# A graph layer and a mixture of experts on one core: the second expert's weights queued behind the fourth node tile's row instead of the first's

## Chip, cores, metric

One NeuronCore of a Trainium2 chip runs the whole program in one launch. The metric is the device time of that launch in microseconds; lower is better. The time before is the median of 3 runs.

## What is computed

625 nodes with 512 features pass a relational graph layer and then a mixture of 16 experts, each with a residual. Cut to what matters:

```python
def gnn(x, heads, tails, rel):               # x = layernorm(input), [625, 512]
    H = einsum('rod,nd->rno', W_rel, x) + b_rel     # 16 relations
    agg = segment_sum(H[rel, tails], heads) + segment_sum(H[rel + 8, heads], tails)
    return relu(x @ W_self.T + b_self + agg)

def moe(x):                                  # x = layernorm(input), [625, 512]
    logits = x @ router_w.T                  # 16 experts
    vals, idx = top_k(logits, 2)
    w = softmax(vals)
    return sum_e w[:, e] * ((silu(x @ gate_w[e]) * (x @ up_w[e])) @ down_w[e])

x = x + gnn(layernorm(x), src, dst, edge_type)
x = x + moe(layernorm(x))
```

There are 10625 edges. One expert has gate and up weights of 512 by 1024 and down weights of 1024 by 512, all float32: 2 MB each, 6 MB together.

## The kernel before

**Node tiles.** The nodes are cut into five tiles of 128 rows, numbered 0 to 4. The graph stage first makes two tables of messages, `h_tab`, with 80 products for each (`relation`, L256), and sorts the edges. Then 128 messages at a time, a chunk, are fetched by index: GpSimd (POOL) issues the indirect DMA at L547 or L553, and TensorE (PE) adds a chunk into its tile with a zero-and-one matrix `to`. Most chunks are split into two parts first (L591 to L595). The last 17 chunks, named `whole` in the code (L614), are multiplied unsplit at L587: three for each of tiles 0 to 3, and five for tile 4. These 17 are the last gathers of the graph stage.

**Finishing a tile.** `finish` (L607) adds the residual (L609, VectorE or DVE), normalizes the row (L148 to L165), stores the normalized tile to `hn_rows` on ScalarE's DMA queue (L611) and stores the tile of `out` on SyncE's (SP's) queue (L612). It keeps that last instruction in the list `stored`. Tiles finish in the order 0, 1, 2, 3, 4. The generator `rest(j)` then routes a tile: four transposes (`pT`, L691), a copy (`hT`, L693), the product with the router (`pl`, L700), the two best experts, and the places of the tile's pairs (L716 to L760). A list of steps written by hand interleaves `finish` and `rest` (L894).

**Experts.** Pairs of a token and an expert are packed into units of 32 tokens. A unit gets its rows by an indirect DMA from `hn_rows`, is transposed on DVE (L788), and runs through gate and up on PE (L800, 32 matmul records for each unit) to `sil` on ScalarE (L812) and `hid` on DVE. The down product is L837, and an indirect DMA adds the result into `out` (L862). Experts 0, 1 and 2 come first, with three units each, called o00, o01, o10, o11, o20, o21, o02, o12, o22 below: the first digit is the expert, the second the unit; PE takes them in this order. Their rows are fetched at L768 by `get_first`: the six of units 0 and 1 once tiles 0 to 3 are routed, the three of unit 2 once tile 4 is. Thirteen more experts follow, in an order found at run time.

**Weights.** Three sets of buffers (`wts0`, `wts1`, `wts2`) take turns, each of 6 MB. `load_hidden` (L173 to L199) and `load_expert` issue three DMAs from SP for an expert: gate, up, down. Expert 0 is loaded during the graph stage. Expert 1 goes to `wts1`, room that the sorting of the edges leaves. Expert 2 goes to `wts2`, room that the graph stage leaves: its load waits until the stage's readers are through, among them the stores of `out` (L612) and `hn_rows` (L611) and the router's last product. Each later expert waits for PE to be done with the set it replaces.

**What sets the place of a load in SP's queue.** `load` takes an instruction from the list `early`, if there is one, and is put behind it by `tc.issue_after`; a scheduler does the rest. Before, `early.extend(3 * stored)` stands ahead of the step list, when `stored` holds tile 0's store alone: expert 1's three loads come right behind it. SP's queue runs in order, and a DMA that SP is to issue can wait for the landing of an older one.

Of the kernel before, what the change touches and what calls it, by code (L numbers as in the profile page):

```python
# [22 lines left out]
NT = 5  # L23
# [51 lines left out]
def kernel(  # L75
# [96 lines left out]
    early = []  # L172

    def load_hidden(e):


        pool = wts[0]
        wts.append(wts.pop(0))

        def load(t, w):  # L180
            s = w[e] if isinstance(e, int) else w[ds(e, 1)].rearrange("o k f -> (o k) f")
            behind = tc.issue_after(early.pop(0)) if early else nullcontext()
            with behind:
                nc.sync.dma_start(t, s.rearrange("(k p) f -> p k f", p=P))

        wgu = pool.tile([P, KD, 2, F], F32, name="wgu")
        load(wgu[:, :, 0, :], gate_w)
        load(wgu[:, :, 1, :], up_w)

        def load_output():  # L190
            wd = pool.tile([P, KF, D], F32, name="wd")
            load(wd, down_w)
            return wd

        return wgu, load_output

    def load_expert(e):
        wgu, load_output = load_hidden(e)
        return wgu, load_output()  # L199
# [3 lines left out]
    with gnn:  # L203
# [401 lines left out]
        stored = []  # L605
# [11 lines left out]
        def add(j, n):  # L617
            for _ in islice(adding[j], n):
                pass
# [46 lines left out]
        weights0 = load_expert(0)  # L666
# [89 lines left out]
        def told_first(units, pairs, all):  # L756

            for c in range(*pairs):
                nc.tensor.matmul(
                    pw0[:, units, :], at[:, c, :], tok0[:, c, units, :], start=(c == 0), stop=(c == all - 1)  # L760
                )

        def get_first(units, tiles):

            nc.vector.tensor_scalar(get0[:, units], pw0[:, units], quarter, 0.0, op0=ALU.add, op1=ALU.max)
            for s in range(NS):
                for g in range(SU)[units]:
                    nc.gpsimd.indirect_dma_start(  # L768
                        out=xb0[:, g, s, :], out_offset=None, in_=hn_quarters[: tiles * P * NQ],
                        in_offset=bass.IndirectOffsetOnAxis(ap=get0[:, g, s : s + 1], axis=0),  # L770
                    )
# [116 lines left out]
        for j in (1, 2, 3):  # L888
            add(j, 3)
        add(0, 3)  # L890

        early.extend(3 * stored)
        weights = [weights0, load_expert(1)]
        for step in ((1, 3), 0, 0, (2, 3), 1, 0, 1, 0, (3, 3), 2, 1, 2, 1, (4, 3), 3, 2, 3, 2, (4, 1), 3, 3):  # L894
            if isinstance(step, int):
                next(tiles[step])
            else:
                add(*step)
        get_first(slice(0, SA), NT - 1)
        told_first(slice(SA, SU), (0, 2 * NT - 2), 2 * NT)  # L900

# [530 lines left out]
```

## Time and profile before

| | |
|---|---|
| median of 3 runs | 725.66 us (722.46 to 725.88) |
| profiled execution, its time | 728.91 us |
| profiled execution, its span | 726.9 us (2.0 us less than its time) |
| PE busy | 676.6 us (93%) |
| DVE busy | 409.0 us (56%) |
| POOL busy | 292.1 us (40%) |
| ScalarE busy | 112.8 us (16%) |
| DMA | 201.13 MB, mean 277 GB/s |
| chain that ended last | PE 74%, DMA 7%, POOL 7%, nothing visible 6% |
| load of gate weights, issue to landing | 19.6 us median |
| L553 gather, issue to landing | 5.3 us median |

The span reaches from the first to the last event of the profiled execution. Matmul ends are modelled and some records are missing, so a PE that is shown busy is not PE at its peak. "Granted clock" is the share of full speed that PE's throttle granted. A timeline row gives start, duration, engine, line, operation and tiles; behind `<-` stands what ended the idle time before it. "Issue to landing" of a DMA counts from the issuing instruction to the DMA's completion.

The stretch that the change touches runs from about 400 us to 480 us: the 17 gathers, the five tiles' finish and routing, and the nine units of experts 0 to 2.

### The profile page before, as it was taken

To read this page: it belongs to the slowest core of one execution; us is meant where nothing else is said; L and a number is where in the kernel's file an instruction comes from. 1 tells how busy PE (TensorE), PEld (TensorE's weight loads), DVE (VectorE), ACT (ScalarE), POOL (GpSimd) and SP (SyncE) were. 2 spreads that over 40 slices of the span, in tenths; PEclk is the share of its full clock that TensorE was granted. 3 is DMA by queue.
4 is the path that set the end of the run, shared out by engine and by line. 5 is a ranking of instruction groups with operands and counts; after the bars stand their busy time and mean duration, and the time that the engine had idled before them with its cause. 6 is when DMAs were issued, how large, how long until landed. Compare 5 with 4: busy or idle time off the path is not lost.

```text
span 726.9 us, 9984 instructions
## 1 busy us (share of the span) xinstructions
PE 676.6 (93%) x3509; PEld 301.4 (41%) x3509; DVE 409.0 (56%) x1106; ACT 112.8 (16%) x218; POOL 292.1 (40%) x263
## 2 busy tenths in 40 slices
PE   4999999999959999999999797999999999999991
PEld 2444444444425555455555253233333333333340
DVE  6569986899249987576887564862222222122210
ACT  2100000000014433233433112111100010001010
POOL 1000004777877770477774713134442222111021
PEclk9999999999979999999999886999999999999996
DMA  7075746999989983689976797579999999999971
GB/s 234 15 270 225 258 144 176 247 269 265 209 257 293 309 271 148 208 270 302 329 244 195 239 404 256 220 268 356 396 383 386 382 395 388 394 396 394 397 253 22
DMA packets 81384, 201.13 MB, mean 277 GB/s; under 512 B 9544, under 2 KB 10226, under 8 KB 81328
## 3 DMA queue, kind: packets, MB, share of 16 engines
q1 hardware_dynamic: 46400, 125.57, 46.4%
q0 software_dynamic: 21712, 52.27, 27.5%
q10 hardware_dynamic: 13216, 22.59, 8.3%
q8 instruction: 29, 0.48, 0.3%
q14 instruction: 27, 0.22, 0.1%
HBM read 175.58 MB, written 27.85 MB: 280 GB/s over the span
## 4 chain that ended last, share of the span: by engine, by line
PE 74%; DMA 7%; POOL 7%; issue 6%; DVE 3%; ACTq 1%; ACT 1%; POOLq 0%; DVEq 0%
PE o L256 25%; PE o L800 24%; PE y L837 12%; POOL agg L547 6%; DMA g<-h_tab,rows 4%; PE m L595 4%; PE m L594 3%; PE m L587 2%; PE ps L494 1%; DMA h_tab<-hs 1%; DMA agg<-h_tab,rows 1%; PE pl L700 1%; DMA wt<-in_w_rel 1%; PE m L564 1%; ACTq L234 1%
## 5 line engine op out<-in xcount | busy, mean ns | idle before, releaser
L256 PE MATMUL o<-wt,xT 128*128 128x512 f32 x680 | 308.4, 599 | 0.7 <-ACT xT L247 0.7
L256 PEld LDWEIGHTS o<-wt,xT 128*128 128x128 f32 x680 | 127.7, 192 | 137.1 <-issue 131.7
L800 PE MATMUL o<-wgu,xbT 128*32 128x512 f32 x1600 | 179.2, 600 | 0.0
L553 POOL DMA_INDIRECT g<-h_tab,rows x142 | 143.6, 1011 | 75.2 <-issue 28.4
L547 POOL DMA_INDIRECT agg<-h_tab,rows x40 | 64.6, 1614 | 133.0 <-DVE off L442 114.1
L591 ACT CAST hi<-g 128x512 fp32r<-128x512 f32 x125 | 71.8, 618 | 224.7 <-DMA g<-h_tab,rows 126.1
L593 DVE TENSOR_TENSOR lo<-g,hi 128x512 fp32r<-128x512 f32 x125 | 82.3, 692 | 35.7 <-ACT hi L591 34.0
L800 PEld LDWEIGHTS o<-wgu,xbT 128*32 128x32 f32 x1600 | 51.8, 111 | 120.8 <-issue 120.4
L788 DVE STREAM_TRANSPOSE xbT<-xb 128x128 f32<-128x128 f32 x50 | 15.1, 307 | 146.7 <-PE o L800 131.2
L837 PE MATMUL y<-wd,hidT 128*32 128x512 f32 (+2 forms) x608 | 92.7, 516 | 0.0
L325 DVE TENSOR_TENSOR hs<-o,bt 128x512 f32<-128x512 f32 x80 | 55.0, 689 | 43.3 <-PE o L256 34.5
L594 PE MATMUL m<-hi,to 128*128 128x512 f32 x125 | 63.5, 508 | 10.0 <-ACT hi L591 10.0
L950 POOL DMA_INDIRECT xb<-hn_rows,get x41 | 39.5, 963 | 57.2 <-DVE xbT L788 32.6
L837 PEld LDWEIGHTS y<-wd,hidT 128*32 128x32 f32 (+2 forms) x608 | 38.7, 128 | 52.1 <-issue 43.9
L595 PE MATMUL m<-lo,to 128*128 128x512 f32 x125 | 55.2, 441 | 1.7 <-DVE lo L593 1.7
L862 POOL DMA_INDIRECT out<-ys,adds x10 | 15.6, 1559 | 76.9 <-ACT ys L857 55.8
L812 ACT ACTIVATE sil<-o 128x256 f32<-128x256 f32 x50 | 19.2, 384 | 150.9 <-PE o L800 146.5
L490 DVE TENSOR_TENSOR val<-oc,vals 128x564 f16<-128x564 f16 (+1 forms) x56 | 38.7, 725 | 0.0
L594 PEld LDWEIGHTS m<-hi,to 128*128 128x128 f32 x125 | 23.9, 191 | 23.8 <-ACT hi L591 13.1
L817 DVE SCALAR_TENSOR_TENSOR hid<-sil,weight,o 128x256 f32<-128x256 f32 x41 | 19.7, 481 | 24.4 <-ACT sil L812 20.7
L595 PEld LDWEIGHTS m<-lo,to 128*128 128x128 f32 x125 | 23.9, 191 | 18.0 <-DVE lo L593 8.9
L474 DVE TENSOR_TENSOR at<-count_h,slot_p 128x768 f16<-128x768 f16 x28 | 26.8, 957 | 0.0
(251 smaller groups left out, 375.5 us busy)
## 6 DMA issues: line engine op xcount, KB each, us to landing
wgu<-in_gate_w SPq DMA_DIRECT2D x16, 2048.0 KB, 19.6
wgu<-in_up_w SPq DMA_DIRECT2D x16, 2048.0 KB, 21.1
wd<-in_down_w SPq DMA_DIRECT2D x16, 2048.0 KB, 23.4
h_tab<-hs ACTq DMA_DIRECT2D x80, 256.0 KB, 4.7
wt<-in_w_rel SPq DMA_DIRECT2D x16, 1024.0 KB, 12.1
bt<-in_b_rel SPq DMA_DIRECT2D x16, 256.0 KB, 12.4
g<-h_tab,rows POOLq DMA_INDIRECT x142, 5.3
xs<-in_x SPq DMA_DIRECT2D x5, 256.0 KB, 5.2
```

The costliest lines, as they stand in the source:

```text
L256: nc.tensor.matmul(o, xT[:, k, ts(j, P)], wt[:, k, :], start=(k == 0), stop=(k == KD - 1))
L325: nc.vector.tensor_tensor(hs, linear(wt, j), bt, ALU.add)
L490: nc.vector.tensor_tensor(val[:, :, i, :], oc, vals[:, cs, i : i + 1].to_broadcast([P, SG, n_ch]), ALU.mult)
L547: nc.gpsimd.indirect_dma_start(out=agg[:, ts(c % NT, D)], out_offset=None, in_=h_tab[d][: n * NP, :], in_offset=at, bounds_check=n * NP - ...
L553: nc.gpsimd.indirect_dma_start(out=g, out_offset=None, in_=h_tab[d][: n * NP, :], in_offset=at,)
L591: nc.scalar.copy(hi, g)
L593: nc.vector.tensor_tensor(lo, g, hi, ALU.subtract)
L594: nc.tensor.matmul(m, at, hi, start=first, stop=False)
L595: nc.tensor.matmul(m, at, lo, start=False, stop=last)
L800: last = nc.tensor.matmul(o[ts(c, Q), :].rearrange("p (s m i) -> p s m i", s=2, i=Q), xbT[:, k, :], wgu[:, k].rearrange("p s (m c i) -> p ...
L837: nc.tensor.matmul(y[at * Q : (at + m) * Q, : cols.stop - cols.start], hidT[:, k, u * Q : (u + m) * Q], wd[:, k, cols], start=(k == 0), st ...
L950: nc.gpsimd.indirect_dma_start(out=xb, out_offset=None, in_=hn_quarters, in_offset=bass.IndirectOffsetOnAxis(ap=get, axis=0),)
```

## The change

Expert 1's loads are no longer traced ahead of the step list. They are traced inside it, once `stored` holds four stores, and are put behind the last of these, tile 3's:

```diff
-
-        early.extend(3 * stored)
-        weights = [weights0, load_expert(1)]
+        weights = [weights0]
         for step in ((1, 3), 0, 0, (2, 3), 1, 0, 1, 0, (3, 3), 2, 1, 2, 1, (4, 3), 3, 2, 3, 2, (4, 1), 3, 3):
             if isinstance(step, int):
                 next(tiles[step])
             else:
                 add(*step)
+            if len(stored) == NT - 1 and len(weights) == 1:
+
+                early.extend(3 * stored[-1:])
+                weights.append(load_expert(1))
```

In the built programs the order of instructions on PE, DVE, ScalarE and POOL is the same. SP's queue alone differs. Before: store of tile 0, gate, up and down of expert 1, stores of tiles 1 to 4, gate, up and down of expert 2. After: stores of tiles 0 to 3, gate, up and down of expert 1, store of tile 4, gate, up and down of expert 2. Some DMAs share a completion semaphore with other ones than before: the stores of tiles 1 to 3 no longer wait for a load of expert 1.

## Prediction

> **What bounds the kernel now.** I read the page first (PE busy 93% of the span), then the chain of work that ended last. From 445 us the chain is PE almost without a break to the end, and the DMA queue's waits say that the later experts' loads wait for PE. So what moves is when PE can run its first nine units. The chain just ahead of them:
>
> ```profile
> 409.35 9.28 DMA g<-h_tab,rows
> 418.68 2.07 PE m L587 x2
> ...
> 445.44 11.27 PE o L800 x80
> 456.85 22.45 PE o L800 x208
> ```
>
> A gather of 256 KB holds PE for 9.28 us. The issue-to-landing times of the L553 gathers, first those issued at 404 to 406 us, then those at 414 to 420 us:
>
> ```profile
> L553 POOL DMA_INDIRECT g<-h_tab,rows x2: 946/1021/1096, 404.2 to 405.6; - x2
> ...
> DMA to landing us min/median/max: 4.8/4.8/4.8
> ...
> L553 POOL DMA_INDIRECT g<-h_tab,rows x5: 942/946/946, 414.4 to 419.4; - x5
> ...
> DMA to landing us min/median/max: 10.6/10.9/11.7
> ```
>
> What came between is in SP's timeline: expert 1's 6 MB.
>
> ```profile
> 407.19 0.36 SPq L612 DMA_DIRECT2D out<-xs  x1
> 408.20 0.38 SPq L184 DMA_DIRECT2D wgu<-in_gate_w  x1
> ...
> 444.01 0.39 SPq L184 DMA_DIRECT2D wgu<-in_gate_w  x1
> 444.45 0.50 SPq L184 DMA_DIRECT2D wgu<-in_up_w  x1
> ```
>
> The table by stretches (the last three columns are granted clock, DMA share, GB/s) shows the same from PE's side: starved, then throttled.
>
> ```profile
> 404.00:408.00 4.00, 3.70 (x9) 1.23 (x8) 2.00 (x5) 0.00 (x0) 2.99 (x3) 1.00 0.60 185
> 408.00:414.00 6.00, 2.08 (x4) 0.42 (x4) 3.23 (x11) 0.31 (x2) 4.68 (x5) 0.92 0.88 275
> 414.00:420.00 6.00, 5.07 (x6) 1.77 (x7) 0.00 (x0) 0.28 (x1) 4.46 (x6) 0.50 0.99 355
> ```
>
> The nine units end one by one at ScalarE's `sil`; the fifth, o20, is the first that needs expert 2:
>
> ```profile
> 462.20 0.38 ACT L812 ACTIVATE sil<-o 128x256 f32<-128x256 f32 x1 [3.05 <-PE o L800]
> 465.63 0.38 ACT L812 ACTIVATE sil<-o 128x256 f32<-128x256 f32 x1 [3.05 <-PE o L800]
> ```
>
> So o20 starts at 462.2. Expert 2's up weights, issued at 444.45, land 16.5 us later (issue-to-landing of that one DMA), at 460.95: only 1.25 us ahead of their use. That small slack decides this case.
>
> **What is removed: the load beside the gathers.** POOL issues the 17 gathers at most 1.25 us apart, whatever the load does. Tile 3's last is the twelfth, issued at 413.11. Uncontended it lands 4.8 us later, at 417.9; its two matmuls take about 1 us (1.13 in the row at 407.83), so tile 3's L609 starts at about 419.3, where it now starts at 425.99: 6.7 us earlier. The bound from below is 3.3 us of landing (the fastest of this stretch: 1.5 us more gain), from above the 9.9 us of the gathers issued near it now (no gain). The value is near the 4.8 of 404 to 406 us, where the DMA share is 0.60. The stores of tiles 1 to 3 move into this time: 0.8 MB. They now wait behind the load (13.6 us of SP's queue for the gate load's landing); afterwards they go as their tiles finish. In the 0.40 of DMA time left, 0.8 MB at 400 GB/s is 2 us of some 13: I cost it at nothing; if it isn't hidden, 1 us.
>
> From tile 3's L609 to tile 4's the trace has 9.85 us (425.99 to 435.84), from there to the first L800 9.5 us (to 445.4). Both are routing in an unchanged instruction order. So PE would be ready for o00 at 419.3 + 9.85 + 9.5 = 438.7.
>
> **What is added: the load beside tile 4 and the first units' rows.** Tile 3's store goes out at about 420.1; gate follows 1.0 us later, as at 407.19 and 408.20; bytes flow from about 422.
> - Tile 4's last gather, issued at 419.37, would land at 424.2 alone and at 431.1 with today's worst 11.7 us. PE reaches it at 434.5 - 6.7 = 427.8. Two or three gathers overlap the load, not ten, so I take 427: cost 0, upper end 3.3 us.
> - The six row gathers of L768, issued now from 440.19 when the queues are nearly empty, landed 2.6 us later (the first). They move to 433.5, into the load. In the stage with 388 GB/s the same kind of gather lands in 6.1 us (median, 520 to 640 us); those beside the start of expert 2's load took 7.9. I take 6.3: 439.8, and o00 at 440.3 instead of 445.4. Of 6.7 us 5.1 are left; by 7.9 us it would be 3.5.
> - Each unit still takes 3.43 us, and o00 its half-clock start. So PE would want o20 at 462.2 - 5.1 = 457.1. Expert 1 itself, wanted at about 450 by o10, is in by then.
>
> **Expert 2, moved by this without being touched.** Its gate load is issued at 444.01, released by the router's last product; SP waited 5.2 us for the store of `hn_rows` just before. It also needs tile 4's store of `out` landed. Now that one takes 5.1 us, issued at 436.6. Afterwards it stands behind expert 1's 6 MB in the same queue. [...] By the 5.1 us, expert 2 would be issued at pl's end, 444.0 - 6.7 = 437.3, and hold nothing: gain 5.1. [...] That end: at 422 there are 6.3 MB of load, 0.6 of gathers, 0.8 of `hn_rows` and 0.4 of rows to move, 8.1 MB; at 400 GB/s (the trace has 400 to 406 from 420 to 438 us) 20.3 us, with a slow start 1 us more: 443.3. The store's 0.26 MB and its completion make 1.5 us, so gate goes out at about 445.0, 1 us later than now. Bounds: 442, if tile 3 comes earlier, and 448.5, if the six small gathers cost the queues 0.8 us each, as they seem to near 450 us.
>
> Up follows 0.4 us later. Now it takes 16.5 us, with three row gathers beside it; two times 2.1 MB at 400 GB/s are 10.5 us, with start and completion 13. The gathers will be through, so I take 15, between them: it lands at 460.4. PE, ready at 457.1, waits 3.3 us, and o20 starts 1.8 us earlier than today.
>
> **After o20** nothing is late: the third rows hang on DVE work behind o10, the next expert's gate load waits 16.5 us for PE at 472.50, and DMA share is 0.03 from 466 to 472 us. Gain and loss at o20 reach the end one to one. On the profiled execution (span 726.9, time 728.91) the sum is 727.1; that one lies 3.25 us above the median, so on the median 725.66 - 1.8 = 723.9.
>
> **Rivals.**
> 1. *Expert 2 is no hindrance.* Its load, with no gathers beside it, lands by 457 (issue 443.5, 13 us). For it: 13 us is what the bytes ask. Against it: today's 16.5. The gain is 5.1 us: 720.6. Chance 0.22.
> 2. *The wait before o20 costs the clock (slower).* [...] A unit then takes 6.9 instead of 3.43 us; half clock over 5 to 10 us loses 2.5 to 5 us. It decides once up lands after about 461 (gate issued after 446). With o20 at 461.7 and 4.5 us lost, 4 us slower: 729.7. Chance 0.20.
> 3. *The gathers don't get faster*, because stores and half a clock hold the tiles, not the load. Then tile 3 stays near 426, the load ends at about 449, up lands near 466, o20 is 3.5 us late: 729.2. The jump from 4.8 to over 10 us right at the load speaks against it. Chance 0.08. That the loads don't move at all is excluded by SP's built order.
>
> **How the numbers follow.** The main case has 0.50. Its own range, from up landing at 458.6 to 463.2, is 722.1 to 726.7. Half a per cent, 3.6 us, is about what a measurement of this kernel can tell from no change. Faster by more than that: rival 1 and the main case's early edge, 0.26. Slower: the larger halves of rivals 2 and 3, 0.19. Within: 0.55. The range reaches from 719.8 (rival 1, tile 3 a little earlier) to 729.0 (the middle of rivals 2 and 3).
>
> **What would show it.** Right: L553 gathers at about 5 us up to 416 us; L609 of tile 3 at 419 to 420 and tile 4 at 429; granted clock full in 414 to 420; first L800 at 440 to 441; tile 4's store landing some 14 us after its issue; expert 2's gate issued at 444 to 446; a PE wait ahead of o20. Wrong: gathers still at 9 us; expert 2's gate at 438 (rival 1 or better); clock 0.50 after 457 (rival 2). A stall elsewhere, such as PE waiting for expert 1 at o10, would make the whole sum wrong.

## The result, and the profile after

The changed kernel takes 729.82 us (median of 15 runs, 726.73 to 731.81). The kernel before took 725.66 us beside it (15 runs, 722.46 to 729.3). The ratio is 1.0052, with an interval of [1.0035, 1.0069]: slower by about 3.8 us (the medians differ by 4.2). The prediction was 723.9 us.

The upper half of the change did what it was meant to do. The L553 gathers of the changed kernel, first those issued at 404 to 413 us, then those at 413 to 418:

```profile
L553 POOL DMA_INDIRECT g<-h_tab,rows x8: 942/946/947, 404.1 to 412.9; - x8
...
DMA to landing us min/median/max: 4.5/4.6/5.0
...
L553 POOL DMA_INDIRECT g<-h_tab,rows x5: 942/946/947, 412.9 to 417.9; - x5
...
DMA to landing us min/median/max: 5.2/5.5/5.8
```

They land in about half the time: the later ones in 5.5 us (median) instead of 10.9. In the table by stretches (columns as before: stretch, its length, busy times of PE, PEld, DVE, ACT and POOL, then granted clock, DMA share, GB/s) PE is busy 4.52 us of the six in which it had been starved, and keeps its full clock:

```profile
408.00:414.00 6.00, 4.52 (x13) 1.88 (x14) 2.61 (x7) 0.29 (x1) 4.59 (x5) 1.00 0.86 284
414.00:420.00 6.00, 5.19 (x23) 2.65 (x22) 4.38 (x22) 1.47 (x3) 3.78 (x4) 1.00 0.95 320
```

The gain is then lost at one place. ScalarE's `sil` marks the end of each unit; o11, the last that needs no weights of expert 2, and o20, the first that does:

```profile
455.47 0.38 ACT L812 ACTIVATE sil<-o 128x256 f32<-128x256 f32 x1 [3.05 <-PE o L800]
468.24 0.38 ACT L812 ACTIVATE sil<-o 128x256 f32<-128x256 f32 x1 [12.39 <-PE o L800]
```

o11 ends 6.7 us earlier than before, o20 2.6 us later (1.5 us of both is that this execution came to tile 0 sooner, see below). PE's timeline splits these 12.8 us into a wait of 6.5 and a unit that takes 6.3 in place of 3.4:

```profile
439.11 10.87 PE L800 MATMUL o<-wgu,xbT 128*32 128x512 f32 x80 [0.87 <-DVE xbT L788]
...
450.04 5.36 PE L800 MATMUL o<-wgu,xbT 128*32 128x512 f32 x48
461.92 18.27 PE L800 MATMUL o<-wgu,xbT 128*32 128x512 f32 x144 [6.52 <-DVE hid L815]
```

The releaser named in the last row is doubtful: `hid` of o11 ended at 461.80, but the up weights of expert 2 landed at 461.78 (the last of the trace's semaphore marks for that DMA), and in the profiles below the same row names `in_up_w`. In g2, below, o20 starts at 453.93, though `hid` of o11 ends only at 458.26: it does not wait for it. Short stretches around the wait show the clock:

```profile
453.40:457.00 3.60, 2.00 (x20) 0.39 (x12) 0.98 (x3) 0.38 (x1) 1.17 (x1) 1.00 1.06 394
457.00:460.40 3.40, 0.00 (x0) 0.00 (x0) 2.63 (x9) 0.00 (x0) 0.00 (x0) 1.00 1.04 267
460.40:463.80 3.40, 1.88 (x12) 0.65 (x16) 1.95 (x4) 0.00 (x0) 0.00 (x0) 0.50 0.93 349
463.80:467.20 3.40, 3.40 (x24) 0.88 (x19) 0.00 (x0) 0.00 (x0) 0.00 (x0) 0.50 0.38 146
```

And SP's timeline shows why expert 2 is late:

```profile
405.71 14.13 SPq L612 DMA_DIRECT2D out<-xs  x4
420.03 0.39 SPq L184 DMA_DIRECT2D wgu<-in_gate_w  x1
420.48 0.60 SPq L184 DMA_DIRECT2D wgu<-in_up_w  x1
...
429.35 4.78 SPq L612 DMA_DIRECT2D out<-xs  x1
445.20 0.37 SPq L184 DMA_DIRECT2D wgu<-in_gate_w  x1
445.62 0.50 SPq L184 DMA_DIRECT2D wgu<-in_up_w  x1
```

Four stores, then expert 1's load, then tile 4's store at 429.35, and expert 2's gate only at 445.20. What SP waited for just before it (us in total, times, longest), and that one store's issue-to-landing:

```profile
SPq L184 <- DMA out<-xs: 5.6, 1, 5.6
```

```profile
L612 SPq DMA_DIRECT2D out<-xs x1: 4776/4776/4776, 429.4 to 429.4; - x1
...
DMA to landing us min/median/max: 15.6/15.6/15.6
```

**How profiles are compared here.** One execution differs from the next by a few us. Two things make the traces comparable. From the ninth `sil` to the end of the span every profile below, those of a slower chip left out, has 247.3 to 247.9 us, so nothing differs there. And tile 0's L609, ahead of which nothing of the change lies, starts anywhere from 402.9 to 408.2 us. What matters is the stretch between these two points: 72.9 us before, 77.0 after, which is 4.1 us more; of these the span shows 2.5, because the profiled execution of after happened to reach tile 0 1.5 us sooner.

### The profile page after: what moved, and what is told of

Its sections match the earlier page's. It is cut to its first block, busy times and chain, and to the rows that moved or that the text cites. A ratio compares the mean times of both kernels' runs of the same rounds, so it can differ in the third digit from the quotient of the medians.

```text
span 729.4 us, 9981 instructions
## 1 busy us (share of the span) xinstructions
PE 678.3 (93%) x3509; PEld 301.3 (41%) x3509; DVE 409.0 (56%) x1106; ACT 111.9 (15%) x218; POOL 292.8 (40%) x263
## 5 line engine op out<-in xcount | busy, mean ns | idle before, releaser
L800 PE MATMUL o<-wgu,xbT 128*32 128x512 f32 x1600 | 181.6, 606 | 7.4 <-DVE hid L815 6.5
L553 POOL DMA_INDIRECT g<-h_tab,rows x142 | 143.6, 1011 | 76.2 <-issue 27.4
L800 PEld LDWEIGHTS o<-wgu,xbT 128*32 128x32 f32 x1600 | 52.4, 112 | 130.1 <-issue 121.4
L862 POOL DMA_INDIRECT out<-ys,adds x10 | 15.6, 1559 | 76.7 <-ACT ys L857 55.7
L490 DVE TENSOR_TENSOR val<-oc,vals 128x564 f16<-128x564 f16 (+1 forms) x56 | 38.5, 720 | 0.0
```

The costliest lines, as they stand in the source:

```text
L490: nc.vector.tensor_tensor(val[:, :, i, :], oc, vals[:, cs, i : i + 1].to_broadcast([P, SG, n_ch]), ALU.mult)
L553: nc.gpsimd.indirect_dma_start(out=g, out_offset=None, in_=h_tab[d][: n * NP, :], in_offset=at,)
L800: last = nc.tensor.matmul(o[ts(c, Q), :].rearrange("p (s m i) -> p s m i", s=2, i=Q), xbT[:, k, :], wgu[:, k].rearrange("p s (m c i) -> p ...
```

## The experiments

My theory after the result: expert 2's load waits for tile 4's store, which stands behind expert 1's 6 MB in SP's queue; the load lands late; PE's wait then halves the clock. The rivals: something else holds expert 2 (the row gathers of the third units, which now fall into its load, or the chip's limit), or the clock is innocent.

| run | edit to the changed kernel | median us (runs) | ratio to before | stretch us | PE's wait ahead of o20, us |
|---|---|---|---|---|---|
| after | none | 729.82 (15) | 1.0052 [1.0035, 1.0069] | 77.0 | 6.52 |
| g1 | none, again | 731.70 (7) | 1.0058 [1.0026, 1.0091] | 74.6 | 4.60 |
| e1 | tile 4's store on ScalarE's queue | 720.12 (11) | 0.9937 [0.9907, 0.9966] | not used | |
| g2 | the same, again | 722.99 (7) | 0.9941 [0.9914, 0.9968] | 68.5 | 0.76 |
| e3 | third units' rows later | 727.58 (22) | 1.0028 [1.0011, 1.0045] | 72.2 | 2.82 |
| g4 | store and rows | 720.55 (6) | 0.9908 [0.9886, 0.9930] | 67.6 | 0.38 |
| e2 | o20 filled twice | 730.14 (8) | 1.0055 [1.0029, 1.0081] | 77.1 | none |
| g3 | o20 filled once | 727.78 (12) | 1.0022 [0.9997, 1.0048] | 72.2 | 1.34 |
| e4 | the kernel before, store on ScalarE's queue | 726.31 (14) | 1.0010 [0.9984, 1.0036] | 71.6 | none |

The e runs shared one chip (before: 725.79 us, 42 runs), the g runs another (726.17 us, 19 runs). By their profiles the stretch of one kernel scatters by 2.4 us (77.0 and 74.6 for the changed kernel), so the ratios carry the verdicts and the traces the reasons.

**Take the store out of SP's queue (e1, g2).**

```
-            stored.append(nc.sync.dma_start(out[ts(j, P), :], xs[:, j, :]).ins)
+            queue = nc.scalar if j == NT - 1 else nc.sync
+            stored.append(queue.dma_start(out[ts(j, P), :], xs[:, j, :]).ins)
```

> The kernel after, with tile 4's store of out issued on ScalarE's DMA queue instead of SP's. Theory (expert 2's load waits for this store, which stands behind expert 1's 6 MB; PE then waits at o20 and its clock halves): the store lands by 440, expert 2's gate is issued at 438 to 440 instead of 445.2, its bytes follow expert 1's without the gap of 444 to 447, up lands at 456 to 458 instead of 461.8, o20 starts there at full clock; 719.5 to 721.5 us. Rival (the loss lies elsewhere, in the gathers or later among the thirteen experts): expert 2 comes earlier, but the time stays within 2 us of 729.8.

Measured 0.9937: faster than both kernels by this one line. The profiled execution of e1 took 730.1 us, ten over its median, so its trace is not read. The trace is that of g2, the same kernel again:

> The changed kernel with tile 4's store of out on ScalarE's queue, to have its trace in an ordinary run. My theory: expert 2's gate is issued at 440 to 442 (tile 4's hn_rows is then what SP waits for), in_up_w lands before 458, no idle time of TensorE over 2 us before o20, no half-clock window after 445, o20's silu at or before 462; time 718 to 722 us, as in the first run. Rival (the store in SP's ring is not what holds expert 2, the third rows' gathers or the chip's limit are): gate issued within 2 us of the changed kernel's, time above 726 us.

Measured 0.9941, with a median of 722.99 us, one us above what was expected. Its SP timeline:

```profile
417.22 0.39 SPq L184 DMA_DIRECT2D wgu<-in_gate_w  x1
...
436.06 0.37 SPq L184 DMA_DIRECT2D wgu<-in_gate_w  x1
436.48 0.50 SPq L184 DMA_DIRECT2D wgu<-in_up_w  x1
```

Its store of tile 4 on ScalarE's queue (the edit moves later lines down by one; the landing times are over those of the five stores of `out` whose landing the trace has, and the longest is tile 4's):

```profile
L613 ACTq DMA_DIRECT2D out<-xs x1: 344/344/344, 426.5 to 426.5; - x1
...
DMA to landing us min/median/max: 4.9/5.0/6.9
```

And PE ahead of o20:

```profile
447.82 5.36 PE L801 MATMUL o<-wgu,xbT 128*32 128x512 f32 x48
453.93 17.37 PE L801 MATMUL o<-wgu,xbT 128*32 128x512 f32 x160 [0.76 <-DMA wgu<-in_up_w]
```

The store lands in 6.9 us instead of 15.6. Counted from tile 0's L609, expert 2's gate is issued at 33.2 us instead of 40.2. PE waits 0.76 us, and five units run in 17.37 us without a half clock. Gate was expected at 440 to 442 and came at 436.06; in the SP waits it is now the store of `hn_rows` that comes last. That the store in SP's queue delays expert 2, and that this turns a gain into a loss, is shown.

**The same edit on the kernel before (e4).** A control: there the store is quick anyway (5.1 us from issue to landing in the kernel before).

> Control: the kernel before, with tile 4's store on ScalarE's DMA queue. Theory (in the kernel before this store has landed before the router's last product releases expert 2's load, so it holds nothing): 725.7 within 1 us. Rival (the other queue for the store is itself what gains): 3 us or more faster.

1.0010: no difference that can be measured. The edit gives nothing of its own; it only takes away what the change had brought in.

**Third units' rows later (e3).** In the changed kernel the three L768 gathers of the third units are issued at 451.2 to 453.7 us, inside expert 2's load; before they were at 461.0 to 463.5, behind the landing of its up weights.

```
-        get_first(slice(SA, SU), NT)
...
-        gated(o11[0], None, hidT0[1], 1)
+        with tc.issue_after(gated(o11[0], None, hidT0[1], 1)):
+            get_first(slice(SA, SU), NT)
```

> The kernel after, with the row gathers of the third units held until o11's hidden rows are made, so that they move from 451 us to 456 or later. Theory (they slow expert 2's up weights while they share the queues): up lands 0.5 to 1.5 us earlier, at 460.3 to 461.3, o20 with it, the half clock stays; 728.3 to 729.3. Rival (they cost nothing, 16 us is what the load takes): 729.8 or more.

1.0028: some 1.7 us better than after, a little more than expected, though the two intervals overlap. Issue to landing of up is 13.6 us, against 14.3 to 16.2 in the four profiles with the gathers inside the load (after, g1, e2, g3). By this one profile the gathers cost the load 0.7 to 2.6 us; since the four differ by 1.9 us among themselves, that is likely and not shown. PE still waits 2.8 us, and the clock falls behind it (0.60 in the row from 460.40):

```profile
457.00:460.40 3.40, 0.71 (x8) 0.00 (x0) 3.23 (x11) 0.38 (x1) 0.78 (x1) 0.90 1.01 373
460.40:463.80 3.40, 3.27 (x20) 1.00 (x24) 1.25 (x9) 0.00 (x0) 2.05 (x3) 0.60 1.05 400
463.80:467.20 3.40, 3.40 (x36) 1.09 (x32) 1.10 (x4) 0.38 (x1) 0.00 (x0) 1.00 0.33 89
```

**Keep PE busy in the wait (e2, g3).** o20's gate and up products (32 matmul records, 3.4 us; the expectation of g3 calls them 28 steps) are run n times beforehand with expert 1's weights; the real ones then begin the sums anew, so this is added work whose result is dropped. n is 2 in e2 and 1 in g3.

```
         o20 = begun(2, 0)
+        for _ in range(n):
+            steps(range(KD), (o20[0], weights[1][0], o20[2]))
         steps(range(KD), o20)
```

> The kernel after, with PE kept busy while it waits for expert 2: o20's rows are first multiplied twice with expert 1's weights into the same buffer (6.9 us of work that the real o20 overwrites). Theory (half clock, not the wait alone, is what makes it slower than before): o20 starts at about 462.3 at full clock and ends 2.6 us earlier than in the kernel after; 726.5 to 727.5 us. Rival (the clock costs nothing here, the wait does): 729.8 to 730.5.

e2 measured 1.0055, no better than after, and missed what was expected. The clock did stay full from 444.7 us on (1.00 in every row from 445 to 490), but the filling ran to about 463.8 us while up had landed at 460.37. The filling took the place of the wait, so this run decides nothing on the clock.

> The changed kernel with o20's 28 steps run once before with expert 1's weights (3.4 us of added TensorE work inside the wait of 6.5 us; the real steps then start the sums anew). If the halved clock behind the wait carries most of the loss: o20 starts within 0.3 us of the changed kernel's and takes 3.4 us in place of 6.3, time 726 to 727.5 us. If the lost gain is the late landing alone and the clock returns elsewhere as much as is saved here: 729 to 731 us.

g3, with half the filling, measured 1.0022 where g1 beside it measured 1.0058: 2.6 us less, though the intervals overlap, so the times alone do not show the clock's part. (Its median, 727.78 us, lies just above the 726 to 727.5 expected.) Its profile is plain. First PE, then the short stretches, of g3:

```profile
448.33 8.79 PE L800 MATMUL o<-wgu,xbT 128*32 128x512 f32 x80
458.46 17.37 PE L800 MATMUL o<-wgu,xbT 128*32 128x512 f32 x160 [1.34 <-DMA wgu<-in_up_w]
```

```profile
457.00:460.40 3.40, 2.06 (x24) 0.81 (x24) 2.84 (x8) 0.00 (x0) 0.00 (x0) 1.00 1.02 317
460.40:463.80 3.40, 3.40 (x36) 1.26 (x32) 1.18 (x3) 0.38 (x1) 0.00 (x0) 1.00 0.72 272
```

o20 still waits for up, but starts at full clock and takes 3.7 us to its `sil`; in g1, with up landing 0.7 us later when counted from tile 0's L609, it takes 5.4.

**The changed kernel again (g1).**

> The changed kernel as it is, beside the three below on one chip. If the kernel before is near 726 us there: 729 to 730.5 us, with the second wgu load's in_up_w landing 16 us after its issue, o20's silu about 2.5 us later than in the kernel before, and the clock halved for 6 to 7 us around it.

1.0058, a little slower than expected. In its profile the load is quicker than expected (14.4 us), so PE waits 4.6 us, and one row at half clock follows instead of two:

```profile
457.00:460.40 3.40, 0.58 (x5) 0.20 (x9) 3.32 (x9) 0.00 (x0) 0.00 (x0) 0.96 1.01 268
460.40:463.80 3.40, 3.40 (x24) 1.21 (x20) 0.86 (x3) 0.00 (x0) 0.00 (x0) 0.54 0.93 360
463.80:467.20 3.40, 3.40 (x40) 1.23 (x35) 1.18 (x3) 0.38 (x1) 0.00 (x0) 1.00 0.19 73
```

**Both edits (g4).**

> The store of out on ScalarE's queue and the third units' row gathers put behind gated(o11). If both causes are separate, each gives its part: 717 to 720 us. If with the store gone the load lands early enough anyway, the gathers' move gives nothing: 719 to 722 us, the same as the store's move alone; later gathers could also make the third units late, and then it is above 722 us.

0.9908, 720.55 us: the fastest version of all. The time lies in the range expected if the gathers' move gives nothing (719 to 722 us). Beside g2 (0.9941) the second edit seems to add 2.4 us, but the intervals overlap; in the profiles the stretch differs by 0.9 us. Whether it adds anything is not shown.

**Four runs on a chip that is slower throughout.** There the kernel before took 768.06 us (23 runs).

> The kernel after, with o20's rows first multiplied once with expert 1's weights into the same buffer (3.43 us of work that the real o20 overwrites), so that PE is idle for 2 to 3 us instead of 6.5 ahead of o20, and o20 isn't held by the filling itself. Theory (wait and half clock): o20 starts when up has landed, 460.4 to 462, at full clock; 726.5 to 728 us. Rival (the clock costs nothing beyond the wait): 729.8.

> The kernel after, with tile 4's store on ScalarE's DMA queue and the third units' row gathers held until o11's hidden rows are made. Theory: expert 2's gate at 438 to 440, up lands by 457, o20 starts without a wait of more than 1 us, no half clock behind 450; 718.5 to 721 us, and the profile shows where the 5 us come from. Rival (the 5 us of the store alone came from the state of the chip): 725 or more.

> The kernel after, with PE's order of the nine units changed to o00, o01, o10, o11, o02, o12, o20, o21, o22: expert 2 is wanted 6.9 us of PE work later. Theory (only the wait for expert 2 and its clock stand against the earlier start): PE waits 2 to 3 us for the third rows, none for expert 2, the nine units end at about 475 instead of 482; 721 to 724 us. Rival (the loss lies among the thirteen later experts or in the queues): 728 or more.

> Expert 1's loads behind tile 2's store instead of tile 3's, one step back towards the kernel before. Theory: the load starts at about 415, the gathers of tile 4 land 2 to 4 us later, the first unit starts at 440 to 442, the load ends 3 to 4 us earlier, expert 2's gate goes out at 441 to 443 and up lands at 457 to 460; 724.5 to 727.5 us. Rival (the later the load, the slower, since every later byte is late): between 725.7 and 729.8 in proportion, 728.

f1 and f2 are the kernels of g3 and g4. f3 is the changed kernel with expert 2's three units put last (PE's order o00, o01, o10, o11, o02, o12, o20, o21, o22). f4 hangs the load on the third tile's store:

```
-            if len(stored) == NT - 1 and len(weights) == 1:
+            if len(stored) == NT - 2 and len(weights) == 1:
```

| run | median us (runs) | ratio to before there | span, us | tile 0's L609, us | ninth sil to the end, us |
|---|---|---|---|---|---|
| f1 | 776.83 (6) | 1.0133 [1.0094, 1.0171] | 772.4 | 435.5 | 260.3 |
| f2 | 771.85 (12) | 1.0050 [1.0026, 1.0075] | 768.3 | 430.9 | 261.1 |
| f3 | 776.61 (6) | 1.0116 [1.0085, 1.0147] | 767.8 | 432.6 | 260.3 |
| f4 | 771.80 (12) | 1.0028 [0.9996, 1.0059] | 770.1 | 436.2 | 259.9 |

All four missed. About 30 us are lost ahead of the change and 13 behind it, where no edit reaches. And the stretch that the edits are about has a stop of its own: just ahead of tile 3's L609, DVE stands still for 2.8 us (f3) to 5.9 us (f2) in all four with nothing visible that ends it, and in none of the runs on the other chips. PE then waits up to 3.9 us and, in f1, f2 and f4, runs slower afterwards: the two products of L564 take 2.06 us in each, and 1.10 in f3; f2's granted clock is 0.75 from 440 to 452 us and 0.73 from 452 to 460. From f2, the DVE stop first, then one of 13 gaps of PE behind the stretch, 5.3 us together:

```profile
447.06 0.18 DVE L702 COPY lg<-pl 128x16 f32<-128x16 f32 x1 [5.88 <-remote]
...
521.40 0.58 PE L838 MATMUL y<-wd,hidT 128*64 128x256 f32 x1 [1.02 <-issue]
```

"remote" and "issue" mean that the profile of this core shows nothing that ended the wait. The stretch takes 76.3 us in f2 and 67.6 in g4, the same kernel. On that chip the gain of the two edits does not appear (1.0050 for the kernel that had 0.9908 elsewhere). What stops the engines is open, and so is whether they stop in the kernel before too; no profile of it was taken there. So whether f3's order or f4's earlier place would help on a chip like the other two is not known either.

## Why the prediction was wrong, step by step

The steps counted from tile 0's L609, so that the executions can be compared (the prediction's times less 406.47):

| step | predicted | after | after again (g1) |
|---|---|---|---|
| L609 of tile 3 | 12.8 | 13.8 | 14.3 |
| first L800 | 33.8 | 34.1 | 34.8 |
| o11 done, PE wants o20 | 50.6 | 50.5 | 51.0 |
| gate of expert 2 issued | 38.5 | 40.2 | 40.5 |
| up of expert 2 landed | 53.9 | 56.8 | 55.4 |
| o20's sil | 57.4 | 63.3 | 60.9 |

- **Gathers, tiles, first units: right, in part by luck.** The gathers land in 4.5 to 5.8 us, the clock is full from 408 to 420, and PE wants o20 within 0.4 us of the sum. But tile 3 is 1.0 to 1.5 us late, and the row gathers, taken at 6.3 us, land in 5.3 to 5.9: two errors that mostly cancel. Rival 3 is out.
- **Expert 2 held by the store behind the load: right in kind,** and against rival 1; g2 and e1 show what comes when the store is out of the way, a gain of 4.3 to 4.6 us by the ratios, near rival 1's 5.1. The sum let tile 4's store wait for the end of expert 1's load. That was the author's estimate, and the kernel before shows it in part: its stores issued at 423.67, 428.6 and 432.9 took 16.2, 11.8 and 8.1 us, all landing at 440 to 441, but tile 4's, issued at 436.6, took 5.1. In after tile 4's store took 15.6 us and landed at about 445.0, some 0.8 us behind the load's last landing at 444.1; the sum had 1.5, which no run shows. In size gate came 1.7 to 2.0 us later than the sum. The load took about 2 us longer from gate to the last landing (24.1 in place of 22.2): the summed 400 GB/s held from 426 to 438 us (409 and 403), but there were 300 from 420 to 426 and 212 from 441 to 444.1. That gate's absolute time (445.20, predicted 445.0) agreed is chance, since tile 0 came 1.5 us sooner.
- **"The gathers will be through, so I take 15": the reason was wrong.** The six row gathers of units 0 and 1 are through, but those of the third units come 8.3 us sooner (counted from tile 0) and fall into the load. The prediction moved the units and did not move what hangs on them. The size was 16.2 in one profile and 14.4 in the other, on both sides of 15.
- **"PE, ready at 457.1, waits 3.3 us, and o20 starts 1.8 us earlier": the step that failed.** It priced the wait at its length and put the clock behind it at nothing, leaving that to rival 2. A full-clock o20 that had to wait takes 3.70 us from its start to its `sil` (g2, g3, g4). It took 6.32 after a wait of 6.52 us (after), 5.40 after 4.60 (g1) and 4.98 after 2.82 (e3): a loss of 2.6, 1.7 and 1.3 us. The rows account for it: the half clock lasted 6.8 us in after (460.4 to 467.2), of which o20 used the last 5.3; 3.4 us in g1 (460.1 to 463.5), all of it used; 3.4 us in e3 (459.7 to 463.1), of which 2.6 were used. Half of the used time is the loss, within 0.1 us. For the predicted wait of 3.3 us, between e3's and g1's, that gives 1.3 to 1.7 us (an estimate from these two), which leaves at most 0.5 of the 1.8 us. That a wait of 3.3 us costs no clock was the author's estimate, and no run shows it: a half clock followed the waits of 2.82 us (e3), 4.60 (g1) and 6.52 (after), and none followed 1.34 (g3) or 0.76 (g2). The prediction had a row that warned of it: a clock of 0.50 from 414 to 420 us, behind 2.08 busy us of six.

The sum for the profile of after: -1.8 predicted, +1.7 gate, +1.2 landing, +2.6 clock, and 0.4 for an o20 that does not follow another unit without a break (3.70 in place of 3.43) and for release: +4.1, which is the measured difference of the stretch. For g1: -1.8 + 2.0 - 0.6 + 1.7 + 0.4 = +1.7, as measured. The +3.8 of the ratio lies between. So the clock is the term that had no price, and the end of expert 1's load is one that was mis-sized by about as much in g1.

Rival 2 was the right outcome, given a chance of 0.20. That its 729.7 us is so near the measured 729.82 is partly luck: it had o20 start 0.5 us earlier than before and lose 4.5 us to the clock, where in after o20 started 1.2 us later and lost 2.6. Its condition, up landing after about 461, was met: with tile 0 where the prediction had it, up landed at 463.3 in after and 461.8 in g1. That line was the author's estimate, which no run shows, and it was drawn too late: e3, at 459.8, lost clock too.

- **After o20 nothing is late: right.** The 247.3 to 247.9 us behind the ninth `sil` are the same in every profile but those of the slower chip.
- **Smaller misreadings, of no weight in the sum.** POOL's gathers are at least 1.25 us apart, not at most (up to 1.68 us early in the 17). The 9.28 us of the chain is a gather's time from issue to landing; PE stood still for only 0.87 us just before 418.68. And a landing of 9.9 us would by the same sum still have left a gain of 1.6 us at tile 3, not none.

## What to carry to other kernels

When a bulk load moves, list what is issued behind it in the same queue and what waits for that: here a store of 0.26 MB behind 6 MB (15.6 us to its landing, 6.9 on another queue) held back the next load, and the one line that puts it on another queue decides between 0.5% slower and 0.6% faster. Price a wait of TensorE twice, by its length and by the clock that follows (in after 6.5 and 2.6 us). And move everything that hangs on the units that come earlier, small gathers too, before summing up a load that they may fall into.

## What the runs showed of the hardware

- The half clock behind the wait lasted 3.4 us in e3 (459.7 to 463.1) and g1 (460.1 to 463.5), both worked out from the rows above, and 6.8 us in after (460.4 to 467.2). In the 3.4 us just ahead of it PE did nothing in after (457.0 to 460.4), but was busy for 1.4 us in e3 (456.3 to 459.7). Busy time alone does not tell these cases apart: in after the clock stayed at 1.00 behind 3.4 us with 1.8 busy us (453.6 to 457.0, unit products), and was 0.50 behind 3.4 us with 2.4 (426.3 to 429.7, products of the graph stage and of the routing). A wait of 1.34 us (g3) cost no clock.
- A store landed 15.6 us after its issue behind a load in SP's queue (after), and 6.9 us after it on ScalarE's queue (g2), while the same load was running.
- Two chips agree within 0.1% on the kernel before (725.79 and 726.17 us), and a third is 6% slower (768.06), with waits of PE that the profile puts down to nothing. A comparison across chips would have drowned all that is told here.
